# Layer 1 of a graph network takes its overflow tiles first, and x is read back by another queue

## The chip, the core and the metric

The kernel runs on one core of a Trainium2 chip. The metric is the device time of one execution in microseconds (us). The engines are PE (TensorE, the matrix multiplier, whose weight loads are shown apart as PEld), DVE (VectorE), ACT (ScalarE), POOL (GpSimd, which here issues the gathers) and SP (SyncE, which here only issues transfers). Each engine works through its own queue of instructions in order.

## The reference, cut to what matters

Four graph layers follow one another over 12,500 nodes with 128 features and 200,000 edges. Each adds to x what it computes from a normalised x. Only layer 1, an attention over the edges with 8 heads, and the hand-over to layer 2 are touched by the change.

```python
def _L1_gnn_ref(x, edge_vec, edge_length, Wq, bq, Wk, bk, Wv, bv, We1, be1, We2, be2, Wo, bo, ln_g, ln_b, edge_index):
    row, col = (edge_index[0], edge_index[1])
    n = x.shape[0]
    q = (x @ Wq.T + bq).reshape(n, H, HD)
    k = (x @ Wk.T + bk).reshape(n, H, HD)
    v = (x @ Wv.T + bv).reshape(n, H, HD)
    attn = jnp.einsum('ehd,ehd->eh', q[row], k[col]) / math.sqrt(HD)
    edge_bias = jax.nn.silu(edge_length @ We1.T + be1) @ We2.T + be2
    attn = attn + edge_bias
    cut = 0.5 * (jnp.cos(edge_length * math.pi / CUTOFF) + 1.0)
    cut = cut * (edge_length < CUTOFF).astype(jnp.float32)
    attn = attn * cut
    attn_exp = jnp.exp(attn - jnp.max(attn, axis=0, keepdims=True))
    attn_sum = jax.ops.segment_sum(attn_exp, row, num_segments=n)
    attn = attn_exp / (attn_sum[row] + 1e-08)
    out = jax.ops.segment_sum(attn[:, :, None] * v[col], row, num_segments=n)
    out = out.reshape(n, HID) @ Wo.T + bo
    h = x + out
    ...
...
h = jnp.maximum(_layernorm(x, axis=-1), 0.0)
x = x + _L0_gnn_ref(h, edge_index, edge_attr_64, ...)
h = jnp.maximum(_layernorm(x, axis=-1), 0.0)
x = x + _L1_gnn_ref(h, edge_attr_3, edge_weight1, ...)
h = jnp.maximum(_layernorm(x, axis=-1), 0.0)
x = x + _L2_gnn_ref(h, L2_gnn_W, L2_gnn_b, edge_index)
h = jnp.maximum(_layernorm(x, axis=-1), 0.0)
x = x + _L3_gnn_ref(h, src, dst, ...)
```

Here `row` is the source of an edge and `col` its destination. For each node the kernel needs the sum over its edges of `exp(attn) * v[col]` and, beside it, the sum of `exp(attn)`; it divides afterwards.

## The kernel before

**Tiles and blocks.** The nodes lie in 98 blocks of 128. The edges are sorted by their source; a tile is up to 128 edges of one block. Each block owns 16 fixed tiles (`TB = 16`), whatever its number of edges. Edges that do not fit go into 56 overflow tiles (`OV`), and which block an overflow tile belongs to is known only at run time. A step of layer 1 takes `W = 8` tiles, so there are `SV = 196` fixed steps, two for each block, and 7 overflow steps, `NV = 203` in all. Before the change they are taken in the order of their numbers: the fixed steps 0 to 195 and then the overflow steps 196 to 202.

**One step.** `attention` holds the parts of a step as small functions of the step's number `g`:
- `load`: SP fetches the edges' lengths (`near`, 4 buffers) and their places in the block (`lanes`, 3 buffers), spread over the partitions.
- `query`: SP fetches the block's queries. Both steps of a block share one transfer of 128 rows (2 buffers). An overflow step fetches eight, one for each of its tiles, from addresses that it reads from a list (`queries`, one buffer; L1655 and L1656).
- `take`: POOL gathers the keys and values of the edges' other ends, one gather of 128 rows for each tile (L363), into `rows` (10 buffers of 4 tiles, so five steps' worth). In the first step of each block but the last, the first two tiles need no gather: `close_rows` computes them on PE from a table that is kept in SBUF (`choose`, `close_rows`, `close_store`). So even fixed steps have six gathers, odd ones eight, and overflow steps eight.
- `near`, `mine`, `hot`: the edge function's tanh, and the one-hot matrices that spread queries over edges (`mine`) and sum edges into nodes (`hot`).
- `products`: PE computes the edge's bias (`pb`, one PSUM tile of two halves that steps use in turn, `g % 2`) and spreads the queries over the edges (`pq`, 4 buffers).
- `logits`: DVE multiplies queries and keys and adds the bias; ACT takes the exponential (L1752) into one of three `weighted` tiles, `g % 3`.
- `weigh`: DVE multiplies the values by the exponentials (L1762). This is the last reader of `rows`.
- `sums`: for a fixed step PE adds 8 tiles up in one PSUM half (L1773); the 16 matmuls of a block's two steps make one accumulation. For an overflow step each tile is summed by itself (L1778), and DVE adds it to the block's row of `acc`, at an address read from a list (L1780). The two halves of that PSUM tile are used in turn.
- `store`: after the second step of a block DVE copies the sum into `acc` (L1784). `acc` was filled with zeros by POOL earlier, after layer 0 (L2559).

**The order of the work.** `layer1_edges` runs the generator under a manual schedule: each engine's instructions stay in the order in which the loop at L1791 to L1806 emits them. An iteration `i` emits parts of several steps: the loads of step `i + 4`, the queries and gathers of `i + 2`, the weighing and sums of `i - 1`, the products of `i + 1`, the logits of `i`, and so on, each through `step(f, g)`, which skips numbers outside 0 to 202. After every odd iteration `layer1_edges` also emits one step of a background task, `bucket_starts` (L816), which prepares layer 2: its early part counts (L884, four DVE instructions in a step), its late part computes places and lanes (DVE work, a transpose on PE, transfers by SP).

**After the loop.** The largest logit of all edges is found (L756 is the first PE instruction of this), a repair path is skipped, and then layer 2 begins: its x is read back from DRAM by seven transfers of 14 blocks each (`CHUNKS`), which ACT issues (L2585). `layer1_out` (from L1960 on) uses it chunk by chunk: DVE divides the sums (L1967 to L1976), ACT normalises x (`normed`, L352), PE and DVE apply the output projection (L1981 to L1989).

Of the kernel before, what the change touches and what calls it, by code (L numbers as in the profile page):

```python
# [50 lines left out]
ED = D + H + 1  # L51
# [8 lines left out]
W = 2 * G  # L60
# [7 lines left out]
TB = 16  # L68
NS = NB * TB
OV = 56  # L70
NV = (NS + OV) // W
SV = NS // W
# [68 lines left out]
class Net:  # L141
# [1471 lines left out]
    def attention(self, work, psum, kvt, qd, acc, weighted, lists, length, cut, every, near_kv):  # L1613
# [5 lines left out]
        nc = self.nc  # L1619
        idx, place, void, oblocks, obases = lists  # L1620
        lengths, lanes = self.by_tile
        state = [{} for _ in range(NV)]
        wide = [P, W, H]
        pbs = psum.tile([P, 2, W, 2, H], F32, name="pb")
        both = psum.tile([P, 2, 256], F32, name="psum")
# [9 lines left out]
        def at(g):  # L1635
            return slice(g * W, g * W + W)
# [82 lines left out]

        def products(g):  # L1720
            s = state[g]
            pb = s["pb"] = pbs[:, g % 2]
            nc.tensor.matmul(pb.rearrange("p g a h -> p (g a h)"), self.onesb,
                             self.wparts.rearrange("p g a h -> p (g a h)"), start=True, stop=False)
            for j in range(W):
                nc.tensor.matmul(pb[:, j].rearrange("p a h -> p (a h)"), s["near"][:, j * P:(j + 1) * P],  # L1726
                                 self.we.rearrange("p a h -> p (a h)"), start=False, stop=j == W - 1)
            s["pq"] = []
            for i in range(W // G):
                pq = psum.tile([P, G, D], F32, name="pq", bufs=4)  # L1730
                for j in range(G):
                    for h in range(2):
                        nc.tensor.matmul(pq[:, j, :], s["mine"][i][:, j, :],
                                         s["query"][i * G + j][:, h * D:(h + 1) * D], start=h == 0, stop=h == 1)
                s["pq"].append(pq)

        def logits(g):
            s = state[g]
            c, pb = at(g), s["pb"]
            add = work.tile(wide, F32, name="add", bufs=2)  # L1740
            nc.vector.tensor_mul(add, pb[:, :, 0, :], length[:, c, None].to_broadcast(wide))  # L1741
            nc.vector.tensor_add(add, pb[:, :, 1, :], add)
            lg = work.tile(wide, F32, name="lg", bufs=2)
            for i in range(W // G):
                k = s["rows"][i][:, :, :D]
                nc.vector.tensor_mul(k, s["pq"][i], k)
                nc.vector.tensor_reduce(lg[:, i * G:(i + 1) * G, :], k.rearrange("p g (h d) -> p g h d", h=H), axis=AX.X,
                                        op=OP.add)
            nc.vector.tensor_add(lg, lg, add)
            nc.vector.tensor_mul(lg, lg, cut[:, c, None].to_broadcast(wide))  # L1750
            v = s["weighted"] = weighted[g % 3]
            nc.scalar.activation(v[:, :, D:D + H], lg, AF.Exp)  # L1752
            valid = work.tile(wide, F32, name="valid")
            nc.vector.tensor_add(valid, lg, void[:, c, None].to_broadcast(wide))
            nc.vector.tensor_max(every, every, valid)
# [25 lines left out]

        def store(g):
            if g < SV and (g + 1) * W % TB == 0:
                nc.vector.tensor_copy(acc[:, g * W // TB, :ED], state[g]["sum"])  # L1784
            state[g - 1].clear()

        def step(f, g, *a):
            if 0 <= g < NV:
                f(g, *a)

        for i in range(-4, NV + 1):  # L1791
            step(load, i + 4)
            step(query, i + 2)
            step(take, i + 2)
            step(near, i + 2)
            step(weigh, i - 1)
            step(products, i + 1)
            step(close_rows, i + 1)
            step(sums, i - 1)
            step(hot, i, 0)  # L1800
            step(logits, i)
            step(close_store, i + 1)
            step(mine, i + 2)
            step(choose, i + 2)
            step(hot, i, 1)
            step(store, i - 1)  # L1806
            yield
# [592 lines left out]
def gnn(ctx: ExitStack, tc: tile.TileContext, a, out):  # L2400
    nc = tc.nc
# [10 lines left out]
    acc = accopen.enter_context(tc.tile_pool(name="acc", bufs=1, side="right")).tile([P, NB, ED], F32, name="acc")  # L2412
# [17 lines left out]
    with tc.tile_pool(name="x00", bufs=1, side="right") as xpool, tc.tile_pool(name="bin", bufs=1) as pool, \  # L2430
            tc.tile_pool(name="psb", bufs=1, space=PSUM) as psum:
        x = xpool.tile([P, NB, D], F32, name="x")
# [99 lines left out]
    xd_view = xd.rearrange("(b p) d -> p b d", p=P)  # L2532
# [13 lines left out]
    with tc.tile_pool(name="sload", bufs=1) as pool, tc.tile_pool(name="psl", bufs=1, space=PSUM) as psum, \  # L2546
# [4 lines left out]
        for c0, c1 in CHUNKS:  # L2551
            x = work.tile([P, CHUNK, D], F32, name="x", bufs=2)
# [29 lines left out]
                   allow_small_or_imprecise_dtypes=True)  # L2582
    x = xpool.tile([P, NB, D], F32, name="x")
    for lo, hi in CHUNKS:
        nc.scalar.dma_start(x[:, lo:hi, :], xd_view[:, lo:hi, :])  # L2585
    zt, dinv = net.layer2_table(dram, late, x, acc, net.layer1_out(x, ln, acc, eps))
    table = net.layer2_edges(dram, xpool, x, zt, acc, dinv, edges, dbins, (*slists[:2], oblocks), pairs, lanes, places,
                             over)
# [28 lines left out]
```

## Time and profile before

| | us |
|---|---|
| runs, median of five | 9052.46 |
| runs, lowest and highest | 9041.71, 9064.01 |
| profiled execution, its own time | 9020.13 |
| its span (first to last instruction) | 9018.4 |
| busy in the span: PE, DVE, POOL, ACT | 5511.6, 5393.8, 4972.0, 3690.5 |
| layer 1's attention, first gather to last add (2749.4 to 5342.4) | 2593 |
| ACT's first work on x for layer 2 | at 5369.15 |

The profile is of one execution, and its own time is 32 us below the median of the runs, so a stretch of it is compared with other stretches of the same execution. A row of the timeline shows the start and the length in us, the engine, the line, the operation, `output<-input`, the shape and how often it came in a row; in square brackets stands how long the engine had been idle before, and what ended this: the engine, the data and the line. "issue" there means that the profile shows nothing that was waited for. A row of a group shows, after a bar, its busy time in us and the mean of one in ns, and after another the idle time of its engine just before it, and what ended most of that. A row for a line shows how often it ran, its shortest, median and longest duration in ns, and its first and last start. ACTq is ACT's queue, which issues transfers.

### The profile page before, as it was taken

Reading aid. Unit: us, or ns where it says so; the run is one execution under the profiler, and the core shown is the slowest. Engines: PE = TensorE matmul, PEld = TensorE weight load, DVE = VectorE, ACT = ScalarE, POOL = GpSimd, SP = SyncE. Lnnn points to the kernel's source line nnn. Section 1 sums busy time; section 2 is a strip of 40 time slices with the busy share of each in tenths; the row PEclk is TensorE's granted clock in tenths of the full one; section 3 lists DMA queues with packets and bytes.
Section 4 is the critical chain, followed back from the end, with each engine's and each line's share of the span. In section 5 each row is a group of like instructions: output and inputs, shape, how many; then the busy total and the mean of one; then the engine's idle time right before and its main releaser. Section 6 shows DMA issues by size and latency. Waiting matters only on the chain. (4 is left out here: it accounts for less than half of the span.)

```text
span 9018.4 us, 124612 instructions
## 1 busy us (share of the span) xinstructions
PE 5511.6 (61%) x36641; PEld 4207.8 (47%) x36642; DVE 5393.8 (60%) x17358; ACT 3690.5 (41%) x8043; POOL 4972.0 (55%) x5112
## 2 busy tenths in 40 slices
PE   3334433433456666666666653777777777668876
PEld 3233333333335556665656643334444455535555
DVE  5566566666665666555555556555556655667776
ACT  3455555555553222232322225233333434534456
POOL 1666666666634555566655524555555655466652
PEclk7555565555576666676666656898889988889997
DMA  6222222222255444444544432444433333433444
GB/s 111 66 67 65 67 65 69 70 69 67 69 159 164 149 147 146 146 155 151 158 136 137 148 95 57 104 111 114 113 108 100 109 105 112 123 100 107 113 136 116
DMA packets 824916, 993.39 MB, mean 110 GB/s; under 512 B 200981, under 2 KB 593178, under 8 KB 823946
## 3 DMA queue, kind: packets, MB, share of 16 engines
q1 hardware_dynamic: 598287, 543.92, 21.0%
q0 software_dynamic: 183168, 425.79, 17.4%
q10 hardware_dynamic: 42747, 15.32, 0.8%
q8 instruction: 306, 5.01, 0.2%
q14 instruction: 408, 3.34, 0.1%
HBM read 924.13 MB, written 60.39 MB: 109 GB/s over the span
## 5 line engine op out<-in xcount | busy, mean ns | idle before, releaser
L363 POOL DMA_INDIRECT rows<-hw,idxd x1564 | 1485.9, 950 | 1068.5 <-issue 410.9
L363 POOL DMA_INDIRECT rows<-kvt,idxs x1430 | 1400.3, 979 | 1043.4 <-DVE weighted L1762 629.8
L1040 ACT ACTIVATE r<-pout 128x512 f16<-128x512 f32 x2058 | 1191.2, 596 | 1806.9 <-PE sums L999 495.8
L363 POOL DMA_INDIRECT rows<-zt,idxs x1333 | 1288.4, 967 | 1023.9 <-issue 461.5
L999 PE MATMUL sums<-yours,r 128*128 128x494 f16 (+20 forms) x8232 | 1666.0, 327 | 12.0 <-ACT r L1040 7.1
L1037 DVE TENSOR_SCALAR yours<-iotac,bucketp 128x494 f16<-128x494 f16 (+26 forms) x4116 | 1114.5, 320 | 852.4 <-PE sums L999 361.1
L1473 PE MATMUL psum<-rows,weights 128*128 128x130 f32 x3128 | 753.0, 420 | 916.7 <-ACT weights L1467 402.9
L1473 PEld LDWEIGHTS psum<-rows,weights 128*128 128x128 f32 x3128 | 669.7, 316 | 962.7 <-ACT weights L1467 437.6
L999 PEld LDWEIGHTS <-r 128*128 128x128 f16 x8232 | 770.4, 106 | 440.7 <-issue 169.9
L1035 PE MATMUL pout<-z,mine 128*128 128x256 f16 x3136 | 661.5, 299 | 454.4 <-ACT r L1040 222.8
L1773 PE MATMUL psum<-weighted,hot 128*128 128x137 f32 x3136 | 648.7, 351 | 299.5 <-issue 269.8
L363 POOL DMA_INDIRECT rows<-h,late x596 | 596.7, 1001 | 378.7 <-issue 146.0
L1726 PE MATMUL pb<-we,near 128*128 128x16 f32 x3248 | 555.2, 304 | 326.4 <-issue 316.3
L1773 PEld LDWEIGHTS psum<-weighted,hot 128*128 128x128 f32 x3136 | 560.4, 249 | 373.3 <-issue 343.8
L1726 PEld LDWEIGHTS pb<-we,near 128*128 128x128 f32 x3248 | 562.4, 257 | 358.4 <-issue 352.6
L1752 ACT ACTIVATE weighted<-lg 128x64 f32<-128x64 f32 x203 | 53.2, 262 | 1564.7 <-DVE lg L1750 876.3
L1467 ACT ACTIVATE weights<-off,weight,minus 128x128 f32<-128x128 bf16 x1173 | 482.9, 481 | 324.2 <-DVE minus L1457 141.2
L1035 PEld LDWEIGHTS <-mine 128*128 128x128 f16 x3136 | 305.8, 105 | 659.3 <-issue 528.1
L1476 DVE SCALAR_TENSOR_TENSOR acc<-psum,mask,acc 128x130 f32 x782 | 269.9, 345 | 551.9 <-remote 388.6
L1741 DVE TENSOR_TENSOR add<-pb,lengthst 128x64 f32<-128x64 f32 x203 | 45.0, 222 | 823.9 <-remote 588.2
L1021 DVE TENSOR_SCALAR mine<-lanes,lane 128x512 f16<-128x512 f16 x1029 | 377.7, 367 | 97.6 <-PE sums L999 31.9
L2055 DVE TENSOR_SCALAR hot<-iotac,places 128x128 f16<-128x128 f16 x1624 | 351.8, 268 | 131.4 <-PE sums L999 42.9
(549 smaller groups left out, 10018.5 us busy)
## 6 DMA issues: line engine op xcount, KB each, us to landing
near<-lengths SPq DMA_DIRECT2D x203, 512.0 KB
lanes<-lanes SPq DMA_DIRECT2D x392, 256.0 KB
z<-zt SPq DMA_DIRECT2D x441, 128.0 KB
lanes<-slanest SPq DMA_DIRECT2D x203, 256.0 KB
lanes<-dlanes SPq DMA_DIRECT2D x195, 256.0 KB
lanes<-lanes SPq DMA_DIRECT2D x245, 128.0 KB
z<-h SPq DMA_DIRECT2D x196, 128.0 KB
rows<-hw,idxd POOLq DMA_INDIRECT x1564
```

What stands on the lines that cost most here:

```text
L363: self.nc.gpsimd.indirect_dma_start(out=out, out_offset=None, in_=table, in_offset=bass.IndirectOffsetOnAxis(ap=idx[:, t:t + 1], axis=0))
L999: nc.tensor.matmul(sums[i], self.part(r[:, i, :], h), yours[i], start=start and h == 0, stop=stop and h == PARTS - 1)
L1021: nc.vector.tensor_scalar(mine, lane[:, 0 if pairs else s - first, :], self.lane, None, op0=OP.is_equal)
L1035: nc.tensor.matmul(p[:, j, :], mine[:, (i + j) * P:(i + j + 1) * P], z[:, s - first, :], start=True, stop=True)
L1037: nc.vector.tensor_scalar(yours[j], self.iotac[:, :wide[i + j]], place[:, b:b + 1], None, op0=OP.is_equal)
L1040: nc.scalar.activation(r, p, AF.Copy)
L1467: nc.scalar.activation(hot[:, j, :], off, AF.Relu, bias=w[:, j:j + 1], scale=minus[:, j:j + 1])
L1473: nc.tensor.matmul(p, hot[:, j, :], rows[:, j, :n], start=j % G == 0, stop=j % G == G - 1)
L1476: nc.vector.scalar_tensor_tensor(d[:, h, :], p, mask[:, 2 * s + i, h:h + 1], d[:, h, :], op0=OP.mult, op1=OP.add)
L1726: nc.tensor.matmul(pb[:, j].rearrange("p a h -> p (a h)"), s["near"][:, j * P:(j + 1) * P], self.we.rearrange("p a h -> p (a h)"), start=F ...
L1773: nc.tensor.matmul(p, s["hot"][j // G][:, j % G, :], v[:, j, :], start=first and j == 0, stop=last and j == W - 1)
L2055: nc.vector.tensor_scalar(hot, self.iotac[:, :P], place[:, lo + j:lo + j + 1], None, op0=OP.is_equal)
```

## The change

The list `order` names the steps in the order in which they are now taken, the overflow steps 196 to 202 first and the fixed steps 0 to 195 after them; `step` is given the place `i` in this order, and looks up the step. `turns` is the way back, from a step to its place, so that the halves of `pb` and the three `weighted` tiles are still used in turn. `store` no longer copies a block's sum into `acc` but adds it, as overflow tiles may have been added to the block before. The states of steps are cleared in the new order. The seven transfers that read x back for layer 2 are issued by SP (`nc.sync`) and no longer by ACT (`nc.scalar`). The loop over `i` and the background's turn after every odd `i` are as they were.

```diff
--- before.py
+++ after.py
@@ -1620,6 +1620,8 @@
         idx, place, void, oblocks, obases = lists
         lengths, lanes = self.by_tile
         state = [{} for _ in range(NV)]
+        order = [*range(SV, NV), *range(SV)]
+        turns = {g: i for i, g in enumerate(order)}
         wide = [P, W, H]
         pbs = psum.tile([P, 2, W, 2, H], F32, name="pb")
         both = psum.tile([P, 2, 256], F32, name="psum")
@@ -1719,7 +1721,7 @@
 
         def products(g):
             s = state[g]
-            pb = s["pb"] = pbs[:, g % 2]
+            pb = s["pb"] = pbs[:, turns[g] % 2]
             nc.tensor.matmul(pb.rearrange("p g a h -> p (g a h)"), self.onesb,
                              self.wparts.rearrange("p g a h -> p (g a h)"), start=True, stop=False)
             for j in range(W):
@@ -1748,7 +1750,7 @@
                                         op=OP.add)
             nc.vector.tensor_add(lg, lg, add)
             nc.vector.tensor_mul(lg, lg, cut[:, c, None].to_broadcast(wide))
-            v = s["weighted"] = weighted[g % 3]
+            v = s["weighted"] = weighted[turns[g] % 3]
             nc.scalar.activation(v[:, :, D:D + H], lg, AF.Exp)
             valid = work.tile(wide, F32, name="valid")
             nc.vector.tensor_add(valid, lg, void[:, c, None].to_broadcast(wide))
@@ -1781,12 +1783,14 @@
 
         def store(g):
             if g < SV and (g + 1) * W % TB == 0:
-                nc.vector.tensor_copy(acc[:, g * W // TB, :ED], state[g]["sum"])
-            state[g - 1].clear()
-
-        def step(f, g, *a):
-            if 0 <= g < NV:
-                f(g, *a)
+                d = acc[:, g * W // TB, :ED]
+                nc.vector.tensor_add(d, d, state[g]["sum"])
+            if turns[g]:
+                state[order[turns[g] - 1]].clear()
+
+        def step(f, i, *a):
+            if 0 <= i < NV:
+                f(order[i], *a)
 
         for i in range(-4, NV + 1):
             step(load, i + 4)
@@ -2582,7 +2586,7 @@
                    allow_small_or_imprecise_dtypes=True)
     x = xpool.tile([P, NB, D], F32, name="x")
     for lo, hi in CHUNKS:
-        nc.scalar.dma_start(x[:, lo:hi, :], xd_view[:, lo:hi, :])
+        nc.sync.dma_start(x[:, lo:hi, :], xd_view[:, lo:hi, :])
     zt, dinv = net.layer2_table(dram, late, x, acc, net.layer1_out(x, ln, acc, eps))
     table = net.layer2_edges(dram, xpool, x, zt, acc, dinv, edges, dbins, (*slists[:2], oblocks), pairs, lanes, places,
                              over)
```

## The prediction

> **What bounds the kernel now.** I read the page first, then the instructions of the lines that close a step, then the timeline. All differences below are made against the profiled execution (9020.13 us, span 9018.4 us, 1.7 us lie around it) and carried over to the median of the runs, 9052.46 us, which is 32 us above it. A difference under 0.2% (18 us) can't be told from no change here.
>
> ```profile
> L363 POOL DMA_INDIRECT rows<-kvt,idxs x1430 | 1400.3, 979 | 1043.4 <-DVE weighted L1762 629.8
> ...
> L1773 PE MATMUL psum<-weighted,hot 128*128 128x137 f32 x3136 | 648.7, 351 | 299.5 <-issue 269.8
> ```
>
> POOL's gathers wait for DVE's weighing (which frees a buffer of gathered rows), and PE's sums idle 269.8 us although nothing that the profile shows holds them.
>
> ```profile
> L1752 ACT ACTIVATE weighted<-lg x203: 260/262/266, 2801.0 to 5331.0; 128x64 f32<-128x64 f32 x102
> ...
> L1784 DVE COPY acc<-psum x98: 282/292/303, 2824.0 to 5231.6; 128x137 f32<-128x137 f32 x98
> ...
> L1780 DVE TENSOR_TENSOR acc<-acc,psum x56: 296/298/300, 5240.6 to 5342.1; 128x137 f32 x56
> ```
>
> One exponential (L1752) marks a step, so the 203 steps are 203 of them. Fixed steps close a block every (5231.6 - 2824.0) / 97 = 24.82 us, a step every 12.41 us.
>
> ```profile
> 5232.00:5342.00 110.00, 70.94 (x268) 51.72 (x267) 53.78 (x144) 14.65 (x35) 15.58 (x16) 0.50 0.19 58
> ```
>
> This stretch of the windows view holds most of the overflow steps (columns: length, busy PE, its weight loads, DVE, ACT, POOL, PE's clock, DMA share, GB/s). POOL works 15.58 of 110 us: the gathers have run out. The timeline shows a fixed pair of steps:
>
> ```profile
> 3442.23 0.26 ACT L1752 ACTIVATE weighted<-lg 128x64 f32<-128x64 f32 x1 [5.48 <-DVE lg L1750]
> 3443.76 0.53 DVE L884 TENSOR_SCALAR_CACHE_REDUCE bbelow<-bfirst,bleast 128x320 bf16<-128x320 f32 x1
> 3445.99 1.29 DVE L1762 TENSOR_TENSOR weighted<-rows,weighted 128x512 f32<-128x512 f32 x2
> 3457.24 0.22 DVE L1741 TENSOR_TENSOR add<-pb,lengthst 128x64 f32<-128x64 f32 x1 [9.96 <-PE psum L1773]
> 3463.82 1.15 POOL L363 DMA_INDIRECT rows<-kvt,idxs  x1 [8.82 <-DVE weighted L1762]
> ```
>
> POOL issues some 14 gathers in one burst (1.25 us each, 17.5 us), then waits for an even step's weighing. Late in such a burst PE's instructions, each of its normal length, start only 0.7 to 2.8 us apart, until about 2.3 us after the burst; DVE's 9.96 us are a wait for PE in that state. The start of the stage shows it plainest:
>
> ```profile
> 2768.71 0.27 PE L1733 MATMUL pq<-query,mine 128*128 128x128 f16 x2
> 2770.58 0.27 PE L1733 MATMUL pq<-query,mine 128*128 128x128 f16 x1 [1.60 <-issue]
> 2772.68 0.26 PE L1733 MATMUL pq<-query,mine 128*128 128x128 f16 x1 [1.83 <-issue]
> ```
>
> A pair is then quick (17.5 + 3.8 = 21.3 us) or slow (17.5 + 8.9 = 26.4 us). Bursts of 8 (10 us), the overflow steps' own, slowed nothing between 5232 and 5342. So this stage is bound by POOL's bursts and what PE loses under them; overflow steps by a ping-pong of PE and DVE; the stage after it by ScalarE's issue of x.
>
> **The change, part by part.**
>
> *The stage's start.* Five steps of rows are gathered before the first weighing: 34 gathers before (three of the five steps take 6, two take 8), 40 after. First gather 2749.44, first exponential 2801.0: 51.6 us, most of it PE spaced out under the burst. Six more gathers at 1.25 us: +7.5. SP's first step now issues 8 query transfers (0.3 to 0.6 us each) in place of 1, behind the first lengths and lanes; they land by about 2765, before PE is spaced out, so they hide under the burst. If that cover goes, they cost 8 x 0.6 + 2 = 7 us. Bounds +7.5 and +14.5; taken +7.5.
>
> *The overflow steps.* Before, from the last fixed exponential (5212.82) to the last of all (5331.0) 118.2 us lie in seven intervals: 12.3, 27.9 and five of 15.7.
>
> ```profile
> 5268.80 0.26 ACT L1752 ACTIVATE weighted<-lg 128x64 f32<-128x64 f32 x1 [12.41 <-DVE lg L1750]
> 5284.51 0.26 ACT L1752 ACTIVATE weighted<-lg 128x64 f32<-128x64 f32 x1 [12.40 <-DVE lg L1750]
> ```
>
> The queries have one buffer, so SP fetches a step's eight behind PE's products of the step before; in the steady 15.7 us that hides under the eight adds. At the start it doesn't: queries (7 us), products (3), again queries, then eight adds of 1.21 us (9.7) ahead of the next logits. I take the first interval as 30 (nearest row: 27.9; bounds 15.7 and 37) and seven more at 15.7, the last two of which already carry fixed steps: 139.9 us for steps 0 to 8.
>
> *The other 194 intervals.* Of the old fixed intervals the first seven sum to 79.9 (buffers full), the other 188 to 2331.9, so 12.40 each. After the change the first fixed steps again find full buffers, the overflow steps being slower than their gathers: 79.9 for seven. The last four now have no gathers beside them: unhindered steps take 6.9 us, I take 7.5, so 30.0 (bounds 27.6 and 4 x 12.4 = 49.6). The 183 between: 2269.2. In all 2379.1.
>
> *The end.*
>
> ```profile
> 5331.98 1.28 DVE L1762 TENSOR_TENSOR weighted<-rows,weighted 128x512 f32<-128x512 f32 x2
> 5342.10 0.30 DVE L1780 TENSOR_TENSOR acc<-acc,psum 128x137 f32 x1 [0.92 <-PE psum L1778]
> 5342.45 0.38 PE L756 MATMUL ptr<-ident,part 128*8 128x128 f32 x1 [0.39 <-DVE acc L1780]
> ```
>
> Last exponential to L756: 11.45 us, eight adds among them. After: 1.0 to the weighing, its first half, eight matmuls of 0.35 and one add of 0.30: 4.6.
>
> Stage before: 51.6 + 79.9 + 2331.9 + 118.2 + 11.45 = 2593.0. After: 59.1 + 139.9 + 2379.1 + 4.6 = 2582.7. Difference -10.3. The store's copy (292 ns) becomes an add (298): +0.6 over 98. The buffers' turns and the clearing of states issue nothing.
>
> *The beat of the background.* A step of bucket counting runs after every odd iteration. The overflow steps are seven, an odd number, so it now follows an even fixed step's logits and not an odd one's. In some 35 pairs it is DVE work (L884, four times, 2.5 us in all). Before, it delays only the odd weighing, in the middle of a burst; after, it stands ahead of the even weighing, which releases the burst. For it: weighing to weighing shrinks from 8.7 to 6.8 us, and PE gets 2.5 us more without a burst, some 8 instructions of 0.3 that otherwise start at least 0.7 apart, 5.6 us, just above the 5.1 by which slow and quick differ. Today's mean of 24.5 is 37% quick. If all turned quick, 21.3 + 2.5 = 23.8, -0.7 x 35 = -24; if none, +2.5 x 35 = +88, and +1.5 x 23 for the pairs of the bucket placing behind it: +122. Taken: quick pairs +2.5, slow ones -1.5 (four in five turn quick): 0.37 x 2.5 - 0.63 x 1.5 = 0.
>
> *x by SyncE.*
>
> ```profile
> 5352.19 15.63 ACTq L2585 DMA_DIRECT2D x<-xd  x7
> 5361.66 0.21 DVE L2214 TENSOR_SCALAR rdeg<-rdeg 128x98 f32<-128x98 f32 x1
> 5367.85 1.28 ACT L352 ACT_TABLE_LOAD   x1 [23.02 <-DMA x<-xd]
> ```
>
> ScalarE is held 15.63 us by issuing seven transfers; its first real work starts at 5369.15, though the first chunk's packets end at 5356.6. SP has nothing to issue until 5403.33 and meets the same waits. ScalarE can start at some 5358.5 to 5359: -10.2. Later chunks land every 2.7 us at the 345 GB/s seen and are used every 22 us; DVE is busy until 5361.87 and would see its next operands at 5364.5. Taken -10 (bounds -10.5 and 0).
>
> The Trainium skill ("DMA: Bandwidth & Descriptors", section "Issuing engines are not separate DMA queues") says that transfers share the same engines whoever issues them, that another issuer saves sequencer time alone, and that this is usually small beside the transfer. By that "small" x would bring about nothing and the sum would be 9043. The row disagrees on the size: the issue takes 15.63 us and is ahead of the first use.
>
> **The sum.** -10.3 + 0.6 + 0 - 10 = -19.7: 9000 in the profiled execution's terms, 9033 for the median.
>
> **Rivals.**
> - *The beat falls into the gap* (slower). One mechanism: L884 ahead of the even weighing, 2.5 us a pair and nothing won back. It decides from 38 us on, about 1.1 us a pair in 35. For it: the release in the timeline is exactly that weighing. Against it: the 9.96 us of DVE idleness say that PE is late. From half the price (+61) to the whole: 9094 to 9155.
> - *Quick pairs everywhere* (-24): 9009. For it: pairs without L884 take 24.0; against: nothing shows that PE catches up each time.
> - *The start takes what the end gives.* First steps near their upper bounds (+7 and +7) and last four steps at 12.4 (+20): only x remains, 9033 + 34 = 9067. For it: PE was spaced out even after the start's burst; against: no burst runs beside the last four.
> - *x does nothing*, its stage held by something else: 9043. For it: nothing in the rows; against: ScalarE is plainly the late one.
>
> **How the numbers follow.** Chances: forecast 0.50 (own range 9010 to 9060, its beat between -24 and +25), the beat in the gap 0.23, quick everywhere 0.10, start against end 0.12, x in vain 0.05. Faster by over 0.2% is below 9034: half of the forecast's (0.29 with its lower tail), all of quick (0.10), some of the rest (0.04): 0.43. Slower, above 9071: 0.23, half of start against end, a little of the forecast's tail: 0.30. Within: 0.27. The range leaves out about 0.1 on each side: 8988 to 9100.
>
> **What would show it.** First exponential near 58 us after the first gather; first interval near 30, then 15.7; the last four fixed exponentials 7 to 8 us apart; L756 4 to 5 us behind the last; L884 between an even step's exponential and its weighing, with pairs near 24.5 us in that stretch; x's issue on SP and ScalarE's first work 6 to 7 us after it. Wrong, if the pairs with L884 take 26 us or more, if products under overflow steps are spaced out by the gathers beside them, or if steps in which the background does neither counting nor placing change their mean.

## The result and the profile after

The changed kernel took 9073.31 us (median of 26 runs) against 9049.16 us for the kernel before (47 runs): the ratio is 1.0028, with a 95% interval of 1.0020 to 1.0036. It is slower by about 24 us; the forecast was 20 us faster. The profiled execution of the changed kernel took 9046.42 us, with a span of 9044.5 us, 26.1 us above that of before. It lies 27 us below the median of its runs, much as the one of before lay 32 us below.

The page of the changed kernel has these lines in answer to the first ones shown of before (columns as there; its lines stand two further down inside `attention`, so L1764 is the weighing, L1775 the fixed sums, L1754 the exponential; L1787 is the add that replaces the copy at L1784, and behind `attention` lines stand four further down):

```profile
span 9044.5 us, 124595 instructions
...
L363 POOL DMA_INDIRECT rows<-kvt,idxs x1430 | 1397.9, 978 | 1141.7 <-DVE weighted L1764 731.1
...
L1775 PE MATMUL psum<-weighted,hot 128*128 128x137 f32 x3136 | 602.9, 340 | 182.5 <-issue 161.0
```

POOL waits 731.1 us for the weighing where it waited 629.8 us: 101 us more. PE's own idling ahead of the sums fell from 299.5 to 182.5 us. So PE is less in the way at this line, and yet the gathers start later. The start of the stage, by two exponentials:

```profile
2801.99 0.26 ACT L1754 ACTIVATE weighted<-lg 128x64 f32<-128x64 f32 x1 [45.90 <-DVE lg L1752]
2821.51 0.26 ACT L1754 ACTIVATE weighted<-lg 128x64 f32<-128x64 f32 x1 [16.21 <-DVE lg L1752]
```

The first gather is at 2742.0, so the first exponential comes 60.0 us behind it, and the second 19.5 us after the first. The end:

```profile
5366.72 0.26 ACT L1754 ACTIVATE weighted<-lg 128x64 f32<-128x64 f32 x1 [5.91 <-DVE lg L1752]
5373.74 0.26 ACT L1754 ACTIVATE weighted<-lg 128x64 f32<-128x64 f32 x1 [3.70 <-DVE lg L1752]
5380.18 0.26 ACT L1754 ACTIVATE weighted<-lg 128x64 f32<-128x64 f32 x1 [4.26 <-DVE lg L1752]
5386.30 0.26 ACT L1754 ACTIVATE weighted<-lg 128x64 f32<-128x64 f32 x1 [3.94 <-DVE lg L1752]
5391.59 0.30 DVE L1787 TENSOR_TENSOR acc<-acc,psum 128x137 f32<-128x137 f32 x1 [2.82 <-PE psum L1775]
5391.94 0.27 PE L756 MATMUL ptr<-ident,part 128*8 128x128 f32 x1 [0.39 <-DVE acc L1787]
```

The last steps, without gathers beside them, are 6.1 to 7.0 us apart, and L756 follows the last exponential after 5.6 us where it was 11.5. Start and end came out near the sizes worked out. The loss lies between. The spacing of the exponentials, which the trace gives one by one, puts it in one stretch (us; a stretch runs from one numbered exponential to another, in the order in which steps are taken):

| stretch | what is in it | before | after |
|---|---|---|---|
| 0 to 8 | start; overflow steps after the change | 93.0 | 128.4 |
| 8 to 76 | background counts (L884) | 839.1 | 817.8 |
| 76 to 140 | background gathers and small work | 761.6 | 776.8 |
| 140 to 188 | background places buckets (L939 to L957) | 631.4 | 714.4 |
| 188 to 202 | overflow steps before the change; end | 204.8 | 146.8 |

Placing costs 83.0 us more. First and last stretch together gain 22.6, counting gains 21.3, the middle loses 15.2. With the start (+8.4) and the last step (-5.9) the attention is 56.9 us longer. After it, x gives back 21.7 us until the last L1988 matmul. The rest of the kernel, which the change doesn't touch, differs by -9.1 us between the two executions (-7.4 ahead of the attention). 56.9 - 21.7 - 9.1 = 26.1.

The view of waits, over the placing stretch alone and for POOL, names the loss (columns: what waited and for what, us in total, times, longest). Before:

```profile
POOL rows L363 <- DVE weighted L1762: 175.2, 24, 9.6
```

After:

```profile
POOL rows L363 <- DVE weighted L1764: 254.1, 24, 11.7
```

One wait for each pair of steps, 7.3 us before and 10.6 after: 78.9 of the 83 us. The timeline of a pair shows what stands in it. Before:

```profile
4767.19 0.26 ACT L1752 ACTIVATE weighted<-lg 128x64 f32<-128x64 f32 x1 [14.76 <-DVE lg L1750]
...
4769.16 1.28 DVE L1762 TENSOR_TENSOR weighted<-rows,weighted 128x512 f32<-128x512 f32 x2
...
4770.11 1.15 POOL L363 DMA_INDIRECT rows<-kvt,idxs  x1 [7.95 <-DVE weighted L1762]
...
4788.85 0.39 PE L1773 MATMUL psum<-weighted,hot 128*128 128x137 f32 x1 [1.72 <-issue]
```

After:

```profile
4764.49 0.18 PE L1728 MATMUL pb<-we,near 128*128 128x16 f32 x1 [1.91 <-issue]
...
4775.32 0.23 DVE L1743 TENSOR_TENSOR add<-pb,lengthst 128x64 f32<-128x64 f32 x1 [12.87 <-PE pb L1728]
...
4778.99 0.26 ACT L1754 ACTIVATE weighted<-lg 128x64 f32<-128x64 f32 x1 [3.12 <-DVE lg L1752]
...
4780.95 0.28 DVE L939 TENSOR_SCALAR bhit<-bedge,babove 128x128 f32<-128x128 f32 x1
...
4782.35 0.30 PE L957 MATMUL iotap<-ident,bplace 128*128 128x128 f32 x1 [2.05 <-DVE bpart L947]
...
4782.52 1.28 DVE L1764 TENSOR_TENSOR weighted<-rows,weighted 128x512 f32<-128x512 f32 x2
4783.48 1.15 POOL L363 DMA_INDIRECT rows<-kvt,idxs  x1 [11.42 <-DVE weighted L1764]
```

From the even step's exponential to its weighing 1.97 us pass before, and 3.53 after, because the placing's DVE work now stands between (4780.95 to 4782.52). That is 1.56 of the 3.47 us by which POOL's wait grew (7.95 to 11.42) in this pair. In the same place PE's transpose L957 waits 2.05 us for that work, and the products of the next steps are queued behind it. What PE then does in its spaced-out state under the burst also changed: it was the sums of the step just weighed (L1773), it is now the products (L1728) on which the next even step's logits wait.

The stage after the attention:

```profile
5401.20 1.28 ACT L2098 ACT_TABLE_LOAD   x1 [7.18 <-PEq L780]
5401.44 7.04 SPq L2589 DMA_DIRECT2D x<-xd  x4
...
5406.45 1.65 ACT L352 ACTIVATE h<-x,ln,ln 128x128 f32<-128x128 f32 x4 [0.42 <-DMA x<-xd]
```

SP issues at 5401.44, and ScalarE starts on x 5.0 us later, at 5406.45. Counted from L756 that is 14.5 us, against 26.7 before.

### The profile page after: what moved, and what is told of

It reads as the page before. It is cut to its first block, busy times and chain, and to the rows that moved or that the text cites. A ratio compares the mean times of both kernels' runs of the same rounds, so it can differ in the third digit from the quotient of the medians.

```text
span 9044.5 us, 124595 instructions
## 1 busy us (share of the span) xinstructions
PE 5479.7 (61%) x36641; PEld 4191.6 (46%) x36642; DVE 5401.8 (60%) x17358; ACT 3688.1 (41%) x8042; POOL 4962.8 (55%) x5112
## 5 line engine op out<-in xcount | busy, mean ns | idle before, releaser
L363 POOL DMA_INDIRECT rows<-kvt,idxs x1430 | 1397.9, 978 | 1141.7 <-DVE weighted L1764 731.1
L1728 PE MATMUL pb<-we,near 128*128 128x16 f32 x3248 | 567.2, 300 | 479.4 <-issue 469.3
L1728 PEld LDWEIGHTS pb<-we,near 128*128 128x128 f32 x3248 | 576.3, 257 | 513.5 <-issue 498.1
L1775 PE MATMUL psum<-weighted,hot 128*128 128x137 f32 x3136 | 602.9, 340 | 182.5 <-issue 161.0
L1754 ACT ACTIVATE weighted<-lg 128x64 f32<-128x64 f32 x203 | 53.2, 262 | 1486.9 <-DVE lg L1752 755.4
L1775 PEld LDWEIGHTS psum<-weighted,hot 128*128 128x128 f32 x3136 | 530.5, 241 | 242.9 <-issue 215.0
```

Source lines behind the costliest of these rows:

```text
L363: self.nc.gpsimd.indirect_dma_start(out=out, out_offset=None, in_=table, in_offset=bass.IndirectOffsetOnAxis(ap=idx[:, t:t + 1], axis=0))
L1775: nc.tensor.matmul(p, s["hot"][j // G][:, j % G, :], v[:, j, :], start=first and j == 0, stop=last and j == W - 1)
```

## The experiments

The runs came on several chips, and these fall into two kinds, which must be known to read the numbers. On one kind the kernel before takes 9049 to 9208 us, as in the first measurement; on the other 7176 to 7187 us. The difference shows in the traces: on the first kind PE's instructions are spaced out under POOL's bursts, as in the profiles above. Runs of at least four PE starts, each a multiple of 0.70 us (within 0.05) behind the one before, fill 560 us in 80 places in the attention of before, 490 us in 76 places in q1_even, and none in e3_x or e6_after. The clock that the profiled executions show is 0.72 to 0.73 on the first kind and 0.79 to 0.80 on the second. A low clock alone doesn't make the spacing: between 5232 and 5342 the trace of before has a clock of 0.50 and no such run. I call the two kinds spacing and non-spacing chips. Three chips of each kind came after the first measurement, each of them once, so whether the kind belongs to the chip or to the hour isn't shown. A run is compared with the kernel before on its own chip, and stretches only within a kind.

**e1_even, p1_even, q1_even: the changed kernel with the background's old place.** One line in `layer1_edges`:

```diff
-                    if i % 2:
+                    if not i % 2:
```

> The changed kernel with the background's turn after every even iteration, so that it again follows an odd fixed step's logits as before the change; nothing else differs. Theory A (the beat): the loss comes from the stretch in which the background places buckets (exponentials 141 to 189), 714.4 us after the change against 631.4 before; it falls back to 625 to 640, the gap on POOL ahead of an even weighing's gathers from 11.4 to about 8 us; the counting stretch (8 to 76), 817.8 us now, returns to 835 to 840. In sum 83 - 21 + 15 = 77 us less than the changed kernel, if the 64 steps between also return: about 8996 us, and below the kernel before. Rival B (the overflow steps' new place costs, at the start or by the buffers' state): the placing stretch stays near 714 and the time within 10 us of 9073.

> The kernel of e1_even again. On a chip that spaces PE out (kernel before near 9050): theory A says that the placing stretch (140 to 188) falls from 714 to 625 to 640 and counting (8 to 76) rises from 818 to 835 to 840: 9073 - 83 + 21 - 15 = about 9000, 0.5% under the kernel before. Rival B: near 9073. On a chip that doesn't (near 7180): 7167, as in e1_even.

> As p1_even. On a chip that spaces PE out (kernel before near 9050): theory A about 9000, placing (140 to 188) 625 to 640, counting (8 to 76) 835 to 840; rival B near 9073. On one that doesn't: 0.997 of the kernel before, as twice so far.

**e2_flip, p2_flip, q2_flip: the kernel before with the same edit,** so the beat alone.

> The kernel before with the background after every even iteration and nothing else changed: the beat alone. Theory A: the placing stretch grows from 631 to 700 to 715 us, the counting stretch shrinks from 839 to about 818, the time is 9049 + 83 - 21 + 15 = about 9126 us (at least 9100). Rival B: no change beyond 18 us, 9031 to 9067.

> The kernel of e2_flip again: the kernel before with the background after even iterations. On a chip that spaces PE out theory A says 9050 + 83 - 21 + 15 = about 9125, placing 700 to 715, counting near 818. Rival B: 9032 to 9068.

> As p2_flip. On a chip that spaces PE out: theory A about 9125, placing 700 to 715, counting near 818; rival B 9032 to 9068. On one that doesn't: 1.001 of the kernel before, as twice so far.

| run | chip | this, us | before, us | ratio (95%) |
|---|---|---|---|---|
| e1_even | non-spacing | 7166.56 | 7187.05 | 0.9971 (0.9961 to 0.9981) |
| p1_even | non-spacing | 7155.08 | 7176.99 | 0.9971 (0.9959 to 0.9983) |
| q1_even | spacing | 9171.22 | 9207.75 | 0.9954 (0.9935 to 0.9974) |
| e2_flip | non-spacing | 7194.67 | 7187.05 | 1.0013 (1.0004 to 1.0022) |
| p2_flip | non-spacing | 7183.63 | 7176.99 | 1.0010 (1.0001 to 1.0019) |
| q2_flip | spacing | 9251.49 | 9207.75 | 1.0040 (1.0024 to 1.0057) |

The runs on non-spacing chips leave the question open: e1_even's and e2_flip's expectations were times for a chip that spaces PE out. q1_even and q2_flip ran on one, and decide the sign. The beat alone makes the kernel before 44 us slower (about 77 were expected), and taking it back puts the changed kernel 36 us, 0.5%, below the kernel before, as expected; the changed kernel itself was not run on this chip. The stretches say where (us):

| stretch | q2_flip | q1_even | e2_flip | e1_even | e6_after | e3_x |
|---|---|---|---|---|---|---|
| background behind | even | odd | even | odd | even | odd |
| chip | spacing | spacing | non-sp. | non-sp. | non-sp. | non-sp. |
| 8 to 76 | 833.5 | 866.2 | 613.6 | 579.2 | 592.4 | 599.1 |
| 76 to 140 | 800.5 | 803.9 | 611.1 | 615.3 | 612.3 | 617.6 |
| 140 to 188 | 715.9 | 653.1 | 468.1 | 467.3 | 469.8 | 470.1 |

("Even" means that it follows an even fixed step's logits.) On a spacing chip placing costs 63 us more behind an even step (83 in the first pair). Here it is the kernel with the overflow steps last that pays it, so their place isn't what makes it; rival B falls. Counting is 33 us shorter there, as it was by 21 in the first pair. Both of q1_even's stretches are longer than expected (835 to 840, 625 to 640), on a chip on which the kernel before, too, takes 1.8% longer than on the first. The middle stretch doesn't follow the parity (800.5 against 803.9); its 15 us in the first pair are not explained by it. POOL's wait in the placing stretch, q2_flip first, then q1_even:

```profile
POOL rows L363 <- DVE weighted L1762: 254.2, 24, 12.4
```

```profile
POOL rows L363 <- DVE weighted L1764: 196.6, 24, 10.1
```

2.4 us in each of 24 pairs. In these four runs on non-spacing chips placing is 467 to 470 us with either parity. The windows view tells why, before on the spacing chip and then e6_after on the other (length, then busy PE, weight loads, DVE, ACT, POOL with counts, clock, DMA share, GB/s):

```profile
4513.00:5144.00 631.00, 423.77 (x2565) 381.54 (x2566) 346.84 (x933) 171.65 (x374) 352.68 (x362) 0.65 0.46 142
```

```profile
3712.00:4182.00 470.00, 339.50 (x2564) 322.43 (x2565) 350.12 (x935) 175.31 (x383) 358.81 (x366) 0.75 0.64 191
```

In the second, POOL's 358.8 us of work and the 0.30 us behind each of its 366 instructions (110 us) make 469 of 470 us: it never stops, and its total wait for the weighing is

```profile
POOL rows L363 <- DVE weighted L1764: 1.2, 4, 0.3
```

There the gathers set the time, and 3 us more ahead of a weighing are hidden. On a spacing chip PE is late, POOL stops after each burst, and in placing what stands between an even step's logits and its weighing is paid.

**e3_x and e4_order: the two parts of the change apart.** e3_x is the kernel before with x by SP; e4_order is the changed kernel with x by ScalarE.

```diff
-        nc.scalar.dma_start(x[:, lo:hi, :], xd_view[:, lo:hi, :])
+        nc.sync.dma_start(x[:, lo:hi, :], xd_view[:, lo:hi, :])
```

> The kernel before with only x's seven transfers issued by SP. From the trace of the changed kernel (49 us behind at the end of the attention, 27.5 behind at the end of layer 1's output) the move is worth 22 us: about 9027 us. By the prediction's own term it would be 9039; a rival (the 22 us are the wobble of one profile) gives no change, 9040 to 9058.

> The changed kernel with x's transfers back on ScalarE: the order of the steps alone. If the two parts add up: 9073 + 22 = about 9095 us, slower than before by 0.5%. If x's move is worth 10: 9083. If x's move brings nothing: 9073.

**e6_after: the changed kernel itself on such a chip.**

> The changed kernel itself, timed again beside the kernel before on one chip. In the four runs so far the kernel before took 7187 us and not 9049, and no stretch of its layer 1 showed PE instructions spaced 0.7 us apart or more. If this chip is like that: order alone +7 (e4_order) and x alone -26 (e3_x) add up to -19, 7168 against 7187. If it is like the first (kernel before near 9049, PE spaced out): 9073, and the placing stretch near 714 us.

All three came on non-spacing chips. e3_x: 0.9965 (0.9951 to 0.9978), 26 us faster where 22 were expected. e4_order: 1.0009 (1.0000 to 1.0018), 7 us slower, at the edge of the noise; its expectations were times for a spacing chip. e6_after: 0.9980 (0.9971 to 0.9989), 7161.78 against 7176.41, where the two added up to -19: on this chip the change makes the kernel faster, by 15 us. From L756 to the last L1988 the traces give 199.5 to 199.8 us with x on ScalarE (e2_flip, e4_order) and 177.8 to 178.2 with x on SP (e3_x, e6_after), the same 22 us as in the first pair on a spacing chip (199.7 and 178.0). That part doesn't depend on the kind of chip.

**e5_mix, p3_mix, r1_mix: each part of the background at its better parity.**

```diff
-                    if i % 2:
+                    if i % 2 == (i < 110):
```

> The changed kernel with the background after odd iterations up to iteration 109 (counting, as now) and after even ones from 110 on (placing, as before the change). Theory A, on a chip that spaces PE out: counting stays at 818 us, placing falls from 714 to 625 to 640: about 8990, faster than both. On a chip that doesn't: placing was 467.3 to 470.1 with either parity, so within 10 us of the changed kernel. Rival B: as the changed kernel on either.

> The kernel of e5_mix again: changed kernel, background after odd iterations to 109 and even ones from 110. On a chip that spaces PE out theory A says placing 625 to 640 and counting 818: 9073 - 83 = about 8990. Rival B: near 9073.

> As p3_mix. On a chip that spaces PE out: the placing stretch loses the 63 us that parity was worth on the last such chip, counting keeps its shorter form: 1.0028 of the kernel before less 63 / 9050 = 0.9958 of it, and below q1_even's 0.9954 if the counting's 21 to 33 us hold, so 0.992 to 0.996. On one that doesn't: 0.9985, as twice so far.

| run | chip | this, us | before, us | ratio (95%) |
|---|---|---|---|---|
| e5_mix | non-spacing | 7165.84 | 7176.41 | 0.9986 (0.9977 to 0.9995) |
| p3_mix | non-spacing | 7163.59 | 7176.99 | 0.9985 (0.9976 to 0.9994) |
| r1_mix | spacing | 9138.40 | 9207.01 | 0.9937 (0.9916 to 0.9959) |

r1_mix's counting takes 832.2 us and its placing 651.9: the first is that of q2_flip (833.5), the second that of q1_even (653.1), each by its own parity. This is the strongest evidence that the parities act stretch by stretch. Its ratio is within the 0.992 to 0.996 expected; e5_mix, on a chip without the spacing, is within 10 us of the changed kernel (7161.78 there), as expected.

**h1_odd to h4_after_hold: PE held back by an added matmul.** Their expected times are for a non-spacing chip. They came on a spacing one (kernel before 9050.98), so the hold adds to the spacing, and only the differences between these runs can be set against the expectations. The hold, for h1_odd:

```diff
+        def hold(g):
+            if g < SV and g % 2 == 0:
+                r = state[g]["rows"][1]
+                nc.tensor.matmul(bank[:, 500:501], r[:, G - 1, :D], r[:, G - 1, :1], start=True, stop=True)
...
-            step(take, i + 2)
             step(near, i + 2)
             step(weigh, i - 1)
+            step(take, i + 4)
             step(products, i + 1)
             step(close_rows, i + 1)
+            step(hold, i + 4)
```

(`bank` is the PSUM tile of `pb`, made larger.) h2_even adds `not` to the condition, h3_behind moves `yield` to just behind `step(weigh, i - 1)`, and h4_after_hold is h1_odd's edit on the changed kernel.

> On the two chips of the runs so far PE is never spaced out, and pairs of steps last as long as POOL's gathers (16 at 1.25 us = 20 us). Here PE is held on purpose: the kernel before, with one small matmul put ahead of each odd fixed step's sums that reads the last row buffer of the running burst, so that PE gets on only when the burst has landed (for this a step's gathers are emitted two iterations earlier, which leaves POOL's own order of gathers as it was). The output is unchanged. Background after odd iterations, as before. Expected: pairs of 25 to 28 us in place of 18 to 20, near the slow pairs of the first traces; 98 pairs x 7 = 700 us more than the kernel before, 7800 to 8000. If PE catches up in spite of it, under 7400, and the emulation tells nothing.

> h1_odd with the background after even iterations. Theory A (what stands ahead of the even weighing is paid in full once a burst's end and not POOL's number of gathers sets the pair): the placing stretch (exponentials 140 to 188) is longer than h1_odd's by 3.3 us x 21 = 70 us (1.56 for the DVE work, 1.7 for PE's transpose that waits for it), the counting stretch (8 to 76) by up to 2.5 x 34 = 85 us. Rival B (parity doesn't matter, the loss came from the overflow steps): both stretches within 10 us of h1_odd.

> h1_odd with the background's step emitted right behind the even step's weighing (the generator yields after weigh, still on odd iterations). Theory A: the burst is released first, so the placing stretch is as in h1_odd or up to 20 us longer (the odd step's logits come 1.6 us later, under the burst), not 70. Rival C (the background costs the same wherever it stands near an even step): as h2_even.

> The changed kernel (overflow steps first, x by SP, background after odd iterations) with the same hold on PE as h1_odd. Theory A: placing +70 and counting up to +85 against h1_odd as in h2_even, less what start and end save (some 20 us) and 22 us for x: slower than h1_odd by 30 to 115 us, the sign of the first measurement (+24). Rival B: faster than h1_odd by 10 to 25 us, as the changed kernel is beside the kernel before on these chips (7162 against 7176).

| run | this, us | 8 to 76 | 76 to 140 | 140 to 188 |
|---|---|---|---|---|
| h1_odd | 9351.14 | 923.4 | 901.7 | 688.1 |
| h2_even | 9458.13 | 998.5 | 873.8 | 751.5 |
| h3_behind | 9320.21 | 927.3 | 874.8 | 690.2 |
| h4_after_hold | 9460.90 | 998.4 | 876.5 | 752.4 |

POOL's wait over the placing stretch, h1_odd first, then h2_even:

```profile
POOL rows L363 <- DVE weighted L1768: 231.6, 24, 11.5
```

```profile
POOL rows L363 <- DVE weighted L1768: 291.9, 24, 14.5
```

h1_odd and h2_even differ in the parity alone and ran on one chip. With every pair held, theory A's numbers come out: placing +63 (expected 70), counting +75 (expected up to 85), and with the background right behind the weighing instead, +2 and +4. h4_after_hold has h2_even's stretches to within 3 us, and is 110 us slower than h1_odd (expected 30 to 115). In counting the sign is the opposite of that without a hold (+75 here, -21 and -33 there): the 2.2 us a pair of L884 ahead of the weighing are paid when PE is held, and are won back in the pair when it isn't. Why the middle stretch is 25 to 28 us longer in h1_odd than in the other three is not known.

**p4_behind and r2_behind: the changed kernel with the background right behind the even weighing, without a hold.**

```diff
             step(weigh, i - 1)
+            yield
...
             step(store, i - 1)
-            yield
...
-                    if i % 2:
+                    if not i % 2:
```

> The changed kernel with the background's step emitted right behind the even fixed step's weighing (the generator yields behind weigh, on even iterations). On a chip that spaces PE out theory A says placing 625 to 645; counting 800 to 840: 8980 to 9010, below both kernels. If PE's late work under the burst grows by the background's, up to 9040. On a chip that doesn't: 7150 to 7170.

> As p4_behind. On a chip that spaces PE out: placing 625 to 655 as the background no longer stands ahead of the weighing; 0.993 to 0.998 of the kernel before. If its work, now under the burst, makes PE later still: 1.000 to 1.003. On one that doesn't: 1.000, as in p4_behind.

Both were expected to be faster where PE is spaced out, and p4_behind also where it isn't (7150 to 7170); neither is: 7177.42 against 7176.99, 1.0003 (0.9994 to 1.0012), and 9202.39 against 9207.01, 0.9996 (0.9981 to 1.0012); the second interval holds the other case that was named, PE later still. r2_behind's placing takes 689.5 us where 625 to 655 were expected, between r1_mix's 651.9 and q2_flip's 715.9. Behind the weighing the background doesn't delay the burst, but it stands ahead of the odd step's logits: over the placing stretch 12.1 us pass on average from an even exponential to the next odd one, against 7.4 in r1_mix. Only with the hold was that hidden.

## Why the prediction was wrong, by its steps

- **The stage's start**: +7.5 worked out, 60.0 - 51.6 = +8.4 measured. The size is right, and the eight queries were no hindrance. The reason given, PE spaced out under the burst, isn't shown. DVE's first logits start at these rows, before and after:

```profile
2797.34 0.22 DVE L1741 TENSOR_TENSOR add<-pb,lengthst 128x64 f32<-128x64 f32 x1 [28.50 <-remote]
```

```profile
2798.28 0.22 DVE L1743 TENSOR_TENSOR add<-pb,lengthst 128x64 f32<-128x64 f32 x1 [34.31 <-remote]
```

  By the records PE had ended the first step's products at 2765.0 and at 2757.8; the spaced instructions that the prediction shows are the second step's. What ended DVE's wait the profile doesn't tell ("remote"); in both traces it is 5 to 7 us behind the burst's last gather.
- **The overflow steps**: 139.9 us worked out for steps 0 to 8, 128.4 measured. The first interval is 19.5 us, not 30: the second step's queries, of which PE waits for the last until 2801.0, came ahead of the first exponential and didn't hold up the adds as feared. The next six are 15.7 to 18.0, and the eighth, at 8.9 in place of 15.7, helped too.
- **The other 194 intervals**: 2379.1 worked out, 2455.9 measured (2584.3 - 128.4), 76.8 more. The last four fixed intervals, worked out at 30.0, took 29.9 (10.3, 7.0, 6.4 and 6.1). The 183 between were priced at the old mean of 12.40 us; what the flipped parity does to them is the term of the beat, two points below.
- **The end**: 4.6 worked out, 5.6 measured; the 16 matmuls that show as one row take 3.5 us.
- **The beat of the background**: taken at 0, within -24 and +122. This is the step that failed: the traces show -21.3 us in counting and +83.0 in placing, and +15.2 in the stretch between, which the parity doesn't explain. The mechanism was named (the background moves ahead of the weighing that releases the burst), but the two halves were weighed wrongly. Counting was given nearly all the price and has the smaller, opposite effect, near the bound for "all pairs turn quick": its pairs take 24.05 us on average, 24.68 before. L884 does stand ahead of the even weighing, but the even logits come 9.9 us behind the odd ones in place of 16.7, and POOL's total wait for the weighing in this stretch is not longer, before and then after:

```profile
POOL rows L363 <- DVE weighted L1762: 234.1, 37, 12.2
```

```profile
POOL rows L363 <- DVE weighted L1764: 210.3, 33, 10.4
```

  What brings the even logits forward was not tried by itself. Placing was given 0 in the forecast and 1.5 us a pair at most (+34); it cost 3.5 us a pair, +83. The 1.5 counted DVE's work alone. It left out what is queued on PE behind the transpose that waits for that work, although the trace of before has such waits: ahead of 12 of the 21 transposes (L957) PE is idle until DVE's L942, 30.4 us in all. That this second half, some 1.9 us a pair, comes through the transpose is read from the timeline; no run took the transpose away alone.
- **x by SyncE**: -10 worked out, -21.7 measured. ScalarE's start was well estimated (-12.2 from L756, against -10.2). The other 9.5 us lie behind it: the seven chunks' first L1995 rows follow each other every 26.5 us on average before, and every 25.0 after, in another rhythm. Two intervals in ScalarE's timeline, of before and then of after:

```profile
5386.32 5.48 ACT L1995 ACTIVATE inner<-inner,inner,inner 128x128 f32<-128x128 f32 x14
5408.16 5.49 ACT L1995 ACTIVATE inner<-inner,inner,inner 128x128 f32<-128x128 f32 x14
5441.28 5.48 ACT L1995 ACTIVATE inner<-inner,inner,inner 128x128 f32<-128x128 f32 x14
```

```profile
5422.84 5.48 ACT L1999 ACTIVATE inner<-inner,inner,inner 128x128 f32<-128x128 f32 x14
5448.06 5.50 ACT L1999 ACTIVATE inner<-inner,inner,inner 128x128 f32<-128x128 f32 x14 [1.00 <-DVE inner L347]
5472.84 5.50 ACT L1999 ACTIVATE inner<-inner,inner,inner 128x128 f32<-128x128 f32 x14 [0.20 <-DVE inner L347]
```

  Before, they alternate (21.8 and 33.1 us); after, they are even (25.2 and 24.8). Outside `attention` a scheduler orders the instructions, and with the transfers off ScalarE's queue it chose another order there: the square root for `dinv` with its table load now comes first, ahead of x, and the groups of `h` fall differently between the chunks. The prediction took the order as given. e3_x and e6_after have the same even rhythm (25.0 us), so it goes with SP's issuing and not with the order of the steps. That the scheduler's order makes the 9.5 us is argued from the traces; it was not tried by itself.
- **The rivals**: what happened is the first one's mechanism, the beat in the gap, but in the placing and not the counting stretch, and at 77 us in all for the three background stretches (-21.3 + 15.2 + 83.0). Start, overflow steps, end and x make good 42 of it, and 9 are the difference of the untouched rest. That the time came out only 40 us from the forecast is partly luck: the overflow steps and x were each some 12 us better than worked out. x in vain is refuted by e3_x, on a non-spacing chip, and by the traces of the first pair. Start against end is refuted by the trace: the two together gained.
- **The chip**: the forecast took spaced-out PE as given, as the profile of before showed it. On a chip without it the changed kernel is at 0.9980, nearly the ratio forecast (9033 / 9052.46 = 0.9979), but by luck, as the sum is another: the attention is 4 to 6 us longer there (1963 us in e4_order and 1965 in e6_after against e3_x's 1959) and x gives 22.

The Trainium skill ("DMA: Bandwidth & Descriptors", section "Issuing engines are not separate DMA queues") says that starting transfers on several engines at once saves only the sequencer's time for starting them, and calls that usually small beside the transfer. Here this time was 15.63 us on ScalarE's queue; without it ScalarE began 12.2 us earlier, and 22 us came of the move with the new order behind it.

**Versions that beat the kernel before.** The changed kernel with the background behind even iterations (the e1_even edit) is at 0.9971, 0.9971 and 0.9954 of the kernel before, on both kinds of chip. With the split at iteration 110 it is at 0.9937 on a spacing chip. On non-spacing chips the split (0.9986 and 0.9985) doesn't beat the changed kernel, which took 7161.78 us beside its 7165.84, and x by SP alone (e3_x) is as good as any, at 0.9965.

## What to carry to other kernels

When steps are reordered and something else is interleaved by the iteration's number, an odd shift moves it behind a different kind of step; look up which instruction releases the slowest engine's next burst, and what stands ahead of it now. Price such a piece by everything that waits in order behind its waiting instructions, on each engine, not by its own work alone. Ask of each stretch which engine never stops: where it was POOL, the same 3 us cost nothing.

## What was not expected of the hardware

The same kernel takes 7176 to 7187 us on some chips and 9049 to 9208 us on others. In the attention of the slower ones PE starts its instructions on a 0.70 us grid under long bursts of gathers, 560 us of such runs of starts in a 2593 us stage, while each instruction lasts its usual time; on the faster ones the stage takes 1959 us with the kernel before's order and such runs are absent. In the trace of the changed kernel 75 of the 94 bursts of 14 gathers (gathers less than 2 us apart) led to one, which ended some 2.3 us behind the burst in the median; its eight bursts of 6 or 8 led to none. What causes the spacing was not found; the gathers take the same 0.98 us on average, and start the same 1.25 us apart, on both kinds.
